# A four-layer gated cross-attention network: one pair of expert reloads issued later, and three transposes moved between products

## The chip, the cores and the metric

The kernel runs on one core of one Trainium2 chip. Its time is device time in microseconds (us), the median of the runs shown. One execution was also recorded by the hardware profiler; every start time below counts from the first instruction of that execution.

A core has five engines that work side by side and wait for each other through semaphores: TensorE (PE in the profile, with its weight loads shown apart as PEld), VectorE (DVE), ScalarE (ACT), GpSimd (POOL) and SyncE (SP), which here issues nearly all transfers. Each engine takes its instructions in the order in which the program was built.

## The reference, cut to what matters

512 tokens (2 batches of 256) of width 256 go through four layers. Each layer adds a cross attention and a feed-forward, each scaled by the tanh of a gate:

```python
x = x + tanh(g_xattn[0]) * L0_xattn(layernorm(x), ctx)
x = x + tanh(g_ffn[0])   * L0_ffn(layernorm(x), ...)        # ternary weights
x = x + tanh(g_xattn[1]) * L1_xattn(layernorm(x), ctx, Wq, Wk, Wv, Wo)
x = x + tanh(g_ffn[1])   * L1_ffn(layernorm(x), w_gate_up, w_down)
x = x + tanh(g_xattn[2]) * L2_xattn(layernorm(x), ctx, ...) # linear attention
x = x + tanh(g_ffn[2])   * L2_ffn(layernorm(x), router_w, gate_w, up_w, down_w)
x = x + tanh(g_xattn[3]) * L3_xattn(layernorm(x), ctx, mask)
x = x + tanh(g_ffn[3])   * L3_ffn(layernorm(x), ...)        # 8 experts, top 2
```

Three of these stages matter here. L1_xattn has 16 heads of width 128: `softmax(q k^T / sqrt(128)) v`, then `@ Wo`. L3_xattn uses the normed tokens as queries against the context itself. L2_ffn sends each token to one of 8 experts:

```python
max_ind = argmax(sigmoid(x @ router_w), axis=1)
for e in range(8):
    h = silu(x @ gate_w[e]) * (x @ up_w[e])
    out = out + where(max_ind == e, h @ down_w[e], 0)
out = out * max_prob
```

## The kernel before, in words

All 512 tokens stay in `x`, four tiles of 128 tokens by 256. A matrix product on TensorE needs the contracted dimension on the partitions, so each normed tile `xn[:, n, :]` is turned: two transposes by TensorE (one for each half of the width) into a small tile `tr`, and one copy by ScalarE into `xT`. There are two buffers for `tr` (pool `ps_tr`), four for ordinary products (`ps_mm`) and two for sums (`ps_acc`).

The order on an engine is largely written by hand. `inline` (line 222) hangs each instruction behind the last one of the same engine's list, so that inside a stage TensorE (`pe_line`), VectorE (`line`) and GpSimd (`pool_line`) follow the text. What is not in a list, ScalarE above all, is placed by the scheduler of the framework.

A product of two fp32 matrices takes two passes. Where it pays, a product is split into cut operands instead: `three` (line 634) makes four products into `same` (two for each half `k` of the contracted width) and two into `cross`.

**Start of the second layer's attention** (lines 773 to 798). The last two value tiles and head 0's keys are multiplied first, while VectorE and GpSimd make the norms. Then `norm_tiles` turns the four tiles with `turned_x`; after the copy of tile 1 it makes head 1's keys for batch 0 (`whole_keys(1, 0)`, two products of 128x512). Head 1's keys for batch 1 follow after the last tile, and then the queries of heads 0 and 1, which read all of `xT`. Between them ScalarE also carries casts for the context's parts (`context_parts`, line 602), which wait for a cut on VectorE.

**Start of the second layer's feed-forward** (lines 1058 to 1136). Tiles 0 and 1 are turned (`turned1`), then `early_products(0)` multiplies the first context tile for the next layer with `three`, which needs nothing of `xT`. Gate and up products of the first batch follow, then tiles 2 and 3, another `early_products`, and the products of the second batch.

**The third layer's experts** (lines 1558 to 1660). Each group of up to 64 tokens of an expert has a fixed place, and the rest of the tokens go into blocks of 32 whose expert is known only when the kernel runs. Six quads of four blocks are multiplied: `l2_up(q)` makes gate and up, `l2_turn` turns the result into `hT`, and `l2_down(q)` multiplies with the ways down. Quads 0 to 3 use the weights of the fixed experts: eight gate/up slabs `gu2[i]` of 1 MB and eight ways down `dn2[i]` of 512 KB. Once quad q has read its two slabs, SP reloads them for the owner of a later block, and likewise `reload_dn2` the ways down:

```python
for i in {0: [0], 1: [1], 3: [3, 2]}.get(q, []):
    reload_dn2(i)
```

Quad 4 reads `gu2[0..3]` and `dn2[0..3]`, and quad 5 `gu2[4..7]` and `dn2[4..7]`. The loop of line 1637 runs one quad ahead: turn q does `l2_up(q)`, then `l2_down(q - 1)`, then `l2_turn` of q, and then some of the homeward products. `homeward` (line 1633) scatters the rows of quad q back to the tokens of tile n by a product with a mask, `l2_back`, summed over the six quads in `y[0]` (tiles 0 and 1) and `y[1]` (tiles 2 and 3).

**Start of the last layer's attention** (lines 1660 to 1753). After the homeward products `l3_stats(n)` adds `y` to `x` and takes the norm, `norm_apply(n)` makes `xn`, `l3_turned(n)` turns it, and `l3_scores` multiplies it with the context. VectorE's list runs: stats 0, stats 1, xn 0, stats 2, xn 1, two small steps on the mask, stats 3, xn 2, xn 3.

Of the kernel before, what the change touches and what calls it, by code (L numbers as in the profile page):

```python
# [30 lines left out]
M = 512  # L31
# [6 lines left out]
QUADS = 6  # L38
# [12 lines left out]
def flamingo(ctx: ExitStack, tc: tile.TileContext, a: dict, out: bass.AP):  # L51
    nc = tc.nc
# [18 lines left out]
    ctxT = turned_ctx.tile([P, B, 2, M], F32, tag="ctxT", name="ctxT")  # L71
# [40 lines left out]
    def load_group(g):  # L112
        w = pair((0, 1, 2, 0)[g], "w1").rearrange("p s c -> p (s c)")
        nc.sync.dma_start(w, a["l1_all"][g])
        return ([w[:, i * 1024 : (i + 1) * 1024].rearrange("p (k c) -> p k c", k=2) for i in range(3)]
                + [w[:, 3072:4096].rearrange("p (h d) -> p h d", d=D)])
# [8 lines left out]
    l1_w = [load_group(0), load_group(1)]  # L125
# [68 lines left out]
    def behind(i, j, reason):  # L194

        tc.add_manual_dep(i.ins, j.ins.name, mybir.DependencyInfo(
            mybir.DependencyClass.NoSync, mybir.DependencyReason.DATA), reason=reason)

    turn = [0]

# [19 lines left out]
    line, pool_line, pe_line = [], [], []  # L220

    def inline(i, line=line):
        if line:
            if line[-1] is not None:
                behind(i, line[-1], "in the order of the text")
            line[:] = [i]
        return i
# [12 lines left out]
    def norm_apply(n, xn, stats):  # L240
        return inline(nc.vector.tensor_scalar(xn[:, n, :], x[:, n, :], *stats, ALU.subtract, ALU.mult))
# [18 lines left out]
    def tokens(t, n):  # L260
        return t[:, n // 2, :, n % 2 * P : (n % 2 + 1) * P]
# [17 lines left out]
    def mm(shape=None):  # L279
        return ps_mm.tile(shape or [P, 512], F32, tag="mm", name="mm")  # L280
# [238 lines left out]
    for s in range(18):  # L519
        n = s // 4  # L520
        if s < 16:
            es[s] = l0_scores(n, s // 2 % 2, s % 2)
        if 1 <= s <= 16:
            m, i, half = (s - 1) // 4, (s - 1) // 2 % 2, (s - 1) % 2
# [8 lines left out]
        if s == 4:  # L533
            behind(nc.scalar.activation(tg, graw, AF.Tanh), exps[-1], "with the table of exponentials")
            p = ps_l0.tile([P, 2, D], F32, tag="s0", name="tot")
# [42 lines left out]
    HD = 128  # L578
# [52 lines left out]
            held.append(diff)  # L631
        return i

    def three(same, cross, left, right):

        for k in range(2):
            for i in range(2):
                inline(nc.tensor.matmul(same, lhsT=left(i, k), rhs=right(i, k), start=(k == 0 and i == 0), stop=(k == 1 and i == 1)), pe_line)  # L638
        for k in range(2):
            inline(nc.tensor.matmul(cross, lhsT=left(2, k), rhs=right(2, k), start=(k == 0), stop=(k == 1)), pe_line)  # L640
# [22 lines left out]
    def value_tiles():  # L663
        return [q4.tile([P, 2, 512], F32R, tag="q4", name="v_parts") for _ in range(3)]
# [4 lines left out]
    def context_tile(mt):  # L669
        return lambda i, k: ctx_parts[i][:, mt // 4, k, mt % 4 * P : (mt % 4 + 1) * P]  # L670
# [97 lines left out]
    def whole_keys(h, b):  # L768
        p = mm()
        chain(p, [(l1_w[0][1][:, k, h * HD : (h + 1) * HD], ctxT[:, b, k, :]) for k in range(2)])  # L770
        nc.scalar.copy(keys[h][:, b * M : (b + 1) * M], p)
# [4 lines left out]
    keys = {h: q4.tile([P, B * M], F32, tag="q4", name="kT") for h in range(2)}  # L776
    for b in range(B):
        whole_keys(0, b)
    xT = q4.tile([P, B, 2, 256], F32, tag="q4", name="xT")

    def turned_x(n, tr):
        nc.scalar.copy(tokens(xT, n), tr)
        if n == 1:
            whole_keys(1, 0)

    for t in (line, pool_line):
        t.append(None)
# [141 lines left out]
    for h in range(16):  # L929
# [9 lines left out]
        for b in range(B):  # L939
# [24 lines left out]
            if h == 14:  # L964
                if b == 0:
                    w_kv2 = value_tiles()
# [13 lines left out]
            if hl and g < 3:  # L980
                n = 2 * (hl - 1) + b
# [62 lines left out]
    def positives(dst, z, t):  # L1044
        inline(nc.vector.scalar_tensor_tensor(dst, z, 0.0, t, ALU.max, ALU.add))

    def early_products(mt):
        same, cross = (ps_acc.tile([P, 512], F32, tag="acc", name="kv2") for _ in range(2))
        three(same, cross, context_tile(mt), lambda i, k: w_kv2[i][:, k, :])
        return same, cross  # L1050

    def early_keys2(mt, same, cross):
# [7 lines left out]
    def turned1(n):  # L1060
        tr = ps_tr.tile([P, 2, P], F32, tag="tr", name="tr")
        for k in range(2):
            inline(nc.tensor.transpose(tr[:, k, :], xn[:, n, k * P : (k + 1) * P], ident), pe_line)
        nc.scalar.copy(tokens(xT, n), tr)

    for n in range(2):
        turned1(n)
    kv0 = early_products(0)
    early_keys2(0, *kv0)
    norm_apply(2, xn, stats1[2])  # L1070
    early_values2(0, *kv0)
# [93 lines left out]
    ctxT = turned_ctx.tile([P, B, 2, M], F32, tag="ctxT", name="ctxT2")  # L1165
# [8 lines left out]
    dn2 = []  # L1174
# [123 lines left out]
    last = norm_stats(NT - 1)  # L1298
# [165 lines left out]
    last = nc.scalar.activation(prob, lgt, AF.Exp, scale=-1.0)  # L1464
# [42 lines left out]
    for n in range(NT):  # L1507
# [9 lines left out]
    _, owners = nc.values_load_multi_w_load_instructions(  # L1517
        owner_i[0:1, :], engines=[mybir.EngineType.SP], min_val=0, max_val=E - 1,
        skip_runtime_bounds_check_because="a count, cut at 7")
# [39 lines left out]

        return 2 * q + j // 2 if q < 4 else 4 * (q - 4) + j  # L1560

    def reload_dn2(q):
        for i in (2 * q, 2 * q + 1):
            nc.sync.dma_start(dn2[i], a["l2_dn_all"][bass.ds(owners[i], 1), :, :].rearrange("e p c -> (e p) c"))

    def l2_up(q):
        pa, pb = mm(), mm()
# [20 lines left out]
    def l2_down(q, hT):  # L1588
        acc = ps_tr.tile([P, D], F32, tag="tr", name="acc2")
        for c in range(4):  # L1590
            for j in range(4):
                inline(nc.tensor.matmul(acc[j * BLK : (j + 1) * BLK, :], lhsT=hT[:, c, j * BLK : (j + 1) * BLK],  # L1592
                                        rhs=dn2[home(q, j)][:, c * D : (c + 1) * D], start=(c == 0), stop=(c == 3)), pe_line)
        for i in {0: [0], 1: [1], 3: [3, 2]}.get(q, []):
            reload_dn2(i)

        top = q1.tile([P, D], F32, tag="q1", name="top2")
        nc.vector.tensor_scalar(top.bitcast(I32), acc.bitcast(I32), -4096, None, ALU.bitwise_and)
        o = kept_back[q][:, 1, :].rearrange("p (i d) -> p i d", i=2) if q < 4 else q2.tile([P, 2, D], F32R, tag="q2", name="o2")
        nc.scalar.copy(o[:, 0, :], top)  # L1600
        nc.vector.tensor_sub(o[:, 1, :], acc, top)
        return o

    last_back = []
# [28 lines left out]
    def homeward(which):  # L1633
        for q, n in which:
            l2_back(q, os[q], backs[q], y, [n])

    for q in range(QUADS + 1):
        if q < QUADS:
            h = l2_up(q)
        if q == 0:  # L1640
            second_rows()
        if 1 <= q <= QUADS:
            backs[q - 1] = l2_mask(q - 1)
            os[q - 1] = l2_down(q - 1, hTs.pop(q - 1))

        if q == 5:
            dn3 = [load(half, f"l3_dn{k}") for k, half in enumerate(halves_of(5, "dn3"))]
            sh = [load(half, f"l3_sh{k}") for k, half in enumerate(halves_of(0, "sh3"))]
            gu3 = [load(half, f"l3_gu{k}") for k, half in enumerate(halves_of(3, "gu3") + halves_of(4, "gu3"))]
        if q < QUADS:  # L1650
            hTs[q] = l2_turn(h)
        if 2 <= q < QUADS:
            homeward([(q - 2, 0)])
        if q == 5:
            homeward([(0, 1), (1, 1)])
        if q == QUADS:
            homeward([(4, 0), (2, 1), (3, 1), (4, 1)])
            load_table(AF.Exp, silus[0], "the table of exponentials")
    homeward([(5, n) for n in range(2)])
    homeward([(q, n) for q in range(QUADS) for n in (2, 3)])  # L1660
    pe_line.clear()
    late = pair(1, "late").rearrange("p s c -> p (s c)")
    shd = late[:, 0 : 6 * D].rearrange("p (c d) -> p c d", d=D)
# [21 lines left out]
    def l3_stats(n):  # L1685
        add_to_x(n, y[n // 2][:, n % 2, :], c2[:, n : n + 1])
        stats3[n] = norm_stats(n)

    def l3_turned(n):
        tr = ps_tr.tile([P, 2, P], F32, tag="tr", name="tr")  # L1690
        for k in range(2):
            inline(nc.tensor.transpose(tr[:, k, :], xn[:, n, k * P : (k + 1) * P], ident), pe_line)
        nc.scalar.copy(tokens(xT, n), tr)
# [39 lines left out]
    l3_stats(0)  # L1733
    l3_stats(1)
    norm_apply(0, xn, stats3[0])
    l3_stats(2)
    norm_apply(1, xn, stats3[1])
    l3_turned(0)
    p = ps_tr.tile([P, B, 4], F32, tag="tr", name="tr")
    chain(p.rearrange("p b c -> p (b c)"), [(ones, named)])  # L1740
    inline(nc.vector.reduce_sum(none, p, axis=AX.X))
# [66 lines left out]
    sent, returned = [], []  # L1808
# [14 lines left out]
    def scatter(table, index, rows, bound, sent):  # L1823
# [2 lines left out]
        for other in sent:  # L1826
            tc.declare_no_dep(i.ins, other.ins, reason="disjoint rows")
        sent.append(i)

    def after_all(read, sent):  # L1830
        for i in sent:
            tc.add_manual_dep(read.ins, i.ins.name, mybir.DependencyInfo(mybir.DependencyClass.Sync, mybir.DependencyReason.DATA),
                              reason="rows of every scatter are read")

    def send3(s):
        full, t = (small.tile([P, 2, E], F32, tag="full3", name="full3", bufs=4) for _ in range(2))
# [16 lines left out]
    def between(ci, b):  # L1853
        if (ci, b) == (0, 0):
            places(place, base3, sel, halves[0])
            send3(halves[0])
            for n in (2, 3):
                l3_turned2(n)
        if (ci, b) == (1, 0):
            for n in (2, 3):  # L1860
                l3_logits(n)
        return (ci, b) in ((0, 1), (4, 1))
# [132 lines left out]
    rows = []  # L1995
    for n in range(NT):
        o = q2.tile([P, 2, D], F32, tag="q2", name="o3g")
        read = (nc.sync, nc.scalar)[n % 2].dma_start(o, yg[n * 2 * P : (n + 1) * 2 * P, :].rearrange("(p k) d -> p k d", k=2))
# [678 lines left out]
```

## Time and profile before

| what | value |
|---|---|
| median of 3 runs | 552.91 us (552.8 to 553.24) |
| the profiled execution's own time | 553.18 us |
| its span, first to last instruction | 551.4 us |
| granted TensorE clock, mean | 0.999 of full speed |
| TensorE matmul busy | 539.8 us, 98% of the span |
| TensorE weight loads busy | 396.1 us, 72% |
| VectorE busy | 333.4 us, 60% |
| ScalarE busy | 237.9 us, 43% |
| GpSimd busy | 123.6 us, 22% |
| moved by transfers | 60.20 MB, mean 109 GB/s |
| reloads of gate/up slabs | 8 of 1024 KB, issued 424.3 to 443.1 |
| reloads of ways down | 8 of 512 KB, issued 432.3 to 452.0 |

A busy share is an average over stages with different limits. A matmul's end is modelled, so a TensorE row that looks full can hide a wait; the idle time in front of a weight load, with its releaser, shows it better. The profile's chain of waits is followed back from the last instruction, at each step to what released it. A transfer's time to landing counts from its issue and includes what is queued in front of it.

### The profile page before, as it was taken

What the parts mean: (1) busy time and instruction counts of PE and PEld (TensorE: products, weight loads), DVE (VectorE), ACT (ScalarE), POOL (GpSimd) and SP (SyncE); (2) the same over time, 40 slices, a digit from 0 to 9 for tenths busy, and PEclk for the clock granted to TensorE, in tenths of its full rate; (3) what the DMA queues carried; (4) which work ended last, traced back from release to release, by engine and by line L of the source; (5) the groups of instructions that cost most, each with busy time, mean ns of one, the idle gap of its engine ahead of it and who ended that gap; (6) DMA issues with size and microseconds to landing.
All of it is one profiled execution on the core that took longest, in us unless ns stands there. A gap on an engine that the chain in (4) does not pass through costs nothing.

```text
span 551.4 us, 8769 instructions
## 1 busy us (share of the span) xinstructions
PE 539.8 (98%) x3322; PEld 396.1 (72%) x3322; DVE 333.4 (60%) x778; ACT 237.9 (43%) x487; POOL 123.6 (22%) x224
## 2 busy tenths in 40 slices
PE   8999999999999999999999999999999989999995
PEld 6554774888888887887888888687776436984464
DVE  5999888645566454755547658664577424563322
ACT  7885565644354434544443533442324212431320
POOL 4776104111030100301012223301031001252150
PEclk9999999999999999999999999999999999999999
DMA  8910120000004000040001204797041999813013
GB/s 277 428 45 0 45 108 1 1 1 0 1 0 153 0 2 1 1 152 1 0 1 37 117 1 162 271 344 311 1 152 40 385 401 249 317 39 128 20 45 130
DMA packets 16104, 60.20 MB, mean 109 GB/s; under 512 B 2717, under 2 KB 5988, under 8 KB 12422
## 3 DMA queue, kind: packets, MB, share of 16 engines
q1 hardware_dynamic: 14294, 54.76, 27.1%
q0 software_dynamic: 1472, 4.28, 2.2%
q8 instruction: 28, 0.46, 0.3%
q10 hardware_dynamic: 288, 0.52, 0.3%
q14 instruction: 22, 0.18, 0.1%
HBM read 54.75 MB, written 5.25 MB: 109 GB/s over the span
## 4 chain that ended last, share of the span: by engine, by line
PE 84%; DVE 5%; DMA 5%; POOL 1%; issue 1%; ACT 1%; SPq 1%; POOLq 0%; DVEq 0%; ACTq 0%
PE mm L284 26%; PE acc L284 18%; PE mm L638 9%; PE mm L640 4%; PE mm L1571 3%; PE q L638 2%; PE mm L1920 2%; DMA gu<-in_l_gu_all 2%; PE s L464 2%; DMA w<-in_l_gate 2%; PE gu L638 1%; PE acc L476 1%; PE outT L715 1%; PE acc L1592 1%; PE q L640 1%
## 5 line engine op out<-in xcount | busy, mean ns | idle before, releaser
L284 PE MATMUL mm<-qT,kT 128*128 128x256 f32 x256 | 60.7, 381 | 0.0
L284 PE MATMUL acc<-e,v 128*128 128x256 f32 x256 | 60.6, 379 | 0.0
L284 PEld LDWEIGHTS mm<-qT,kT 128*128 128x128 f32 x256 | 48.2, 190 | 9.2 <-ACT oT L823 1.6
L284 PEld LDWEIGHTS acc<-e,v 128*128 128x128 f32 x256 | 48.3, 189 | 8.2 <-issue 0.4
L626 POOL TENSOR_TENSOR h_parts<-w,h_top 128x256 fp32r<-128x256 f32 x28 | 20.8, 743 | 140.0 <-PE acc L284 73.6
L812 ACT ACTIVATE e<-mm 128x512 f32<-128x512 f32 x64 | 38.0, 598 | 22.4 <-PE mm L284 22.2
L815 DVE TENSOR_TENSOR t<-e,e 128x512 f32<-128x512 f32 x32 | 22.1, 690 | 24.4 <-ACT e L812 24.2
L468 ACT ACTIVATE e<-s 128x512 f32<-128x512 f32 x64 | 32.9, 606 | 5.9 <-PE s L464 5.7
L236 POOL TENSOR_TENSOR rstd<-mv,eps_ln 128x1 f32<-128x1 f32 x31 | 6.7, 218 | 110.8 <-DVE mv L235 110.7
L643 ACT ACTIVATE v<-mm 128x512 f32<-128x512 f32 x24 | 14.3, 597 | 31.2 <-PE mm L640 31.2
L638 PE MATMUL mm<-ctx_top,h_parts 128*128 128x512 f32 x56 | 27.4, 489 | 0.0
L284 PE MATMUL acc<-w,oT 128*128 128x256 f32 x112 | 26.8, 381 | 0.1
L823 ACT COPY oT<-acc 128x256 f32<-128x256 f32 x32 | 11.9, 372 | 34.2 <-PE acc L284 34.2
L644 DVE SCALAR_TENSOR_TENSOR v<-mm,v 128x512 f32<-128x512 f32 x24 | 16.6, 691 | 16.6 <-ACT v L643 16.6
L643 ACT ACTIVATE kT<-mm 128x512 f32<-128x512 f32 x28 | 16.7, 597 | 20.6 <-PE mm L640 20.6
L287 DVE SCALAR_TENSOR_TENSOR x<-acc,gsum,x 128x256 f32<-128x256 f32 x56 | 23.6, 476 | 2.8 <-PE acc L284 2.2
L1571 PE MATMUL mm<-gu,xsT 128*32 128x512 f32 x192 | 23.4, 596 | 1.4 <-DMA gu<-in_l_gu_all 1.4
L644 DVE SCALAR_TENSOR_TENSOR kT<-mm,kT 128x512 f32<-128x512 f32 x28 | 19.3, 688 | 6.7 <-ACT kT L643 6.7
L284 PEld LDWEIGHTS acc<-w,oT 128*128 128x128 f32 x112 | 20.1, 190 | 3.5 <-ACT oT L823 0.5
L638 PE MATMUL mm<-v_parts,ctx_top 128*128 128x512 f32 x48 | 22.1, 461 | 0.0
L464 PE MATMUL s<-w_q,ctx_nat 32*128 32x256 f32 x256 | 21.6, 401 | 0.5 <-DVE w_q L424 0.2
L638 PE MATMUL mm<-ctx_rest,h_parts 128*128 128x512 f32 x56 | 22.0, 393 | 0.0
(434 smaller groups left out, 1173.2 us busy)
## 6 DMA issues: line engine op xcount, KB each, us to landing
gu<-in_l_gu_all SPq DMA_DIRECT2D x16, 1024.0 KB, 9.1
w<-in_l_all SPq DMA_DIRECT2D x4, 2048.0 KB, 12.4
dn<-in_l_dn_all SPq DMA_DIRECT2D x4, 1024.0 KB, 6.3
dn<-in_l_dn_all SPq DMA_DIRECT2D x8, 512.0 KB, 7.9
gu<-in_l_gu SPq DMA_DIRECT2D x4, 704.0 KB, 14.9
ctxT<-in_ctxT SPq DMA_DIRECT2D x4, 512.0 KB, 13.4
ctx_nat<-in_ctx SPq DMA_DIRECT2D x3, 512.0 KB, 6.2
dn<-in_l_dn SPq DMA_DIRECT2D x2, 704.0 KB
```

Source lines behind the costliest of these rows:

```text
L284: inline(nc.tensor.matmul(dst, lhsT=lhsT, rhs=rhs, start=(i == 0), stop=(i == len(pairs) - 1)), pe_line)
L287: return inline(nc.vector.scalar_tensor_tensor(x[:, n, cols], acc, scalar, x[:, n, cols], ALU.mult, ALU.add))
L464: in_turn(nc.tensor.matmul(ps[j][:, k, :], lhsT=ctx_nat[rows, b, hf, c * P : (c + 1) * P], rhs=qm[rows, n, i, :], start=True, stop=True))
L468: exps.append(nc.scalar.activation(es[j], ps[j], AF.Exp))
L626: nc.gpsimd.tensor_sub(dst[1], src, t)
L638: inline(nc.tensor.matmul(same, lhsT=left(i, k), rhs=right(i, k), start=(k == 0 and i == 0), stop=(k == 1 and i == 1)), pe_line)
L640: inline(nc.tensor.matmul(cross, lhsT=left(2, k), rhs=right(2, k), start=(k == 0), stop=(k == 1)), pe_line)
L643: nc.scalar.mul(dst, cross, -EPS * scale)
L644: return inline(nc.vector.scalar_tensor_tensor(dst, same, (1.0 + EPS) * scale, dst, ALU.mult, ALU.add))
L812: nc.scalar.activation(e, s, AF.Exp)
L815: nc.vector.tensor_add(t, es[0], es[1])
L1571: inline(nc.tensor.matmul(ps[j * BLK : (j + 1) * BLK, :], lhsT=xsT[k][:, (4 * q + j) * BLK : (4 * q + j + 1) * BLK], rhs=gu2[home(q, j)][: ...
```

## The change

It has four parts.

In the experts' loop, the reload of the second pair of ways down (`dn2[2]`, `dn2[3]`) is taken out of `l2_down(1)` and issued in turn 3 of the loop, after `l2_up(3)` has issued its two slabs. It also gets a dependency: SP waits until the homeward product of quad 1 to tile 0 is done. As built, SP's order becomes slabs 0 to 3, ways down 0 and 1, slabs 4 and 5, slabs 6 and 7, ways down 2 and 3, and then ways down 6, 7, 4 and 5 as before. To write this, `after_all` moves from the last layer to the head of the kernel.

At the end of that loop, the last quad's homeward products to tiles 2 and 3 (four products) are taken out of the list and placed behind the last layer's first turn.

In the second layer's attention, head 1's keys for batch 0 are split into their two products, one after each of the turns 0 and 1; they used to follow turn 1 together. As built, ScalarE's copy of turn 1 stands behind the cast `ctx_top` of line 612 instead of ahead of it.

In the second layer's feed-forward, turn 1 is made inside `early_products(0)`, between the first two and the last two products into `same`, by a new argument `between` of `three`.

VectorE's and GpSimd's orders are the same in both kernels.

```diff
+    def after_all(read, sent):
+        for i in sent:
+            tc.add_manual_dep(read.ins, i.ins.name, mybir.DependencyInfo(mybir.DependencyClass.Sync, mybir.DependencyReason.DATA),
+                              reason="only when these are done")
...
-    def three(same, cross, left, right):
+    def three(same, cross, left, right, between=None):
 
         for k in range(2):
+            if k and between:
+                between()
             for i in range(2):
...
+    keys10 = mm()
+
+    def keys_step(k):
+        inline(nc.tensor.matmul(keys10, lhsT=l1_w[0][1][:, k, HD : 2 * HD], rhs=ctxT[:, 0, k, :], start=(k == 0), stop=(k == 1)), pe_line)
+
     def turned_x(n, tr):
         nc.scalar.copy(tokens(xT, n), tr)
+        if n < 2:
+            keys_step(n)
         if n == 1:
-            whole_keys(1, 0)
+            nc.scalar.copy(keys[1][:, 0:M], keys10)
...
-    def early_products(mt):
+    def early_products(mt, between=None):
         same, cross = (ps_acc.tile([P, 512], F32, tag="acc", name="kv2") for _ in range(2))
-        three(same, cross, context_tile(mt), lambda i, k: w_kv2[i][:, k, :])
+        three(same, cross, context_tile(mt), lambda i, k: w_kv2[i][:, k, :], between)
         return same, cross
...
-    for n in range(2):
-        turned1(n)
-    kv0 = early_products(0)
+    turned1(0)
+    kv0 = early_products(0, partial(turned1, 1))
...
-    def reload_dn2(q):
+    def reload_dn2(q, last=None):
         for i in (2 * q, 2 * q + 1):
-            nc.sync.dma_start(dn2[i], a["l2_dn_all"][bass.ds(owners[i], 1), :, :].rearrange("e p c -> (e p) c"))
+            read = nc.sync.dma_start(dn2[i], a["l2_dn_all"][bass.ds(owners[i], 1), :, :].rearrange("e p c -> (e p) c"))
+            if last is not None:
+                after_all(read, [last])
...
-        for i in {0: [0], 1: [1], 3: [3, 2]}.get(q, []):
+        for i in {0: [0], 3: [3, 2]}.get(q, []):
             reload_dn2(i)
...
         if 2 <= q < QUADS:
             homeward([(q - 2, 0)])
+        if q == 3:
+            reload_dn2(1, last_back[0])
...
     homeward([(5, n) for n in range(2)])
-    homeward([(q, n) for q in range(QUADS) for n in (2, 3)])
+    homeward([(q, n) for q in range(QUADS - 1) for n in (2, 3)])
...
     norm_apply(0, xn, stats3[0])
+    l3_turned(0)
+    homeward([(QUADS - 1, n) for n in (2, 3)])
     l3_stats(2)
     norm_apply(1, xn, stats3[1])
-    l3_turned(0)
...
-    def after_all(read, sent):
-        for i in sent:
-            tc.add_manual_dep(read.ins, i.ins.name, mybir.DependencyInfo(mybir.DependencyClass.Sync, mybir.DependencyReason.DATA),
-                              reason="rows of every scatter are read")
```

## The prediction

> **What bounds the kernel now.** I read the engines' busy shares first, then the chain of waits, then the weight loads' waits in the four places that the change touches, and last the transfers' issues and landings around the third layer's experts. TensorE is nearly the whole chain, so a step is worth what it does to TensorE's next instruction:
>
> ```profile
> PE 84%; DVE 5%; DMA 5%; POOL 1%; issue 1%; ACT 1%; SPq 1%; POOLq 0%; DVEq 0%; ACTq 0%
> ```
>
> The chain in order of time (start, length, what) shows the one transfer in the middle of the kernel:
>
> ```profile
> 438.94 3.64 PE mm L1571 x32
> 443.11 11.03 DMA gu<-in_l_gu_all
> 454.18 2.99 PE mm L1571 x25
> ```
>
> The sixth quad's up products start at 451.12 and wait there for the last reloaded gate/up slab, issued at 443.11, landed 11.03 us later. The timeline of weight loads and of ScalarE (start, length, engine, line, what, idle before and its releaser):
>
> ```profile
> 454.18 0.16 PEld L1571 LDWEIGHTS mm<-gu,xsT 128*32 128x32 f32 x8 [2.35 <-DMA gu<-in_l_gu_all]
> ...
> 460.33 0.58 ACT L206 COPY hT<-tr 128x512 f32<-128x512 f32 x1
> ...
> 460.97 1.45 PEld L1592 LDWEIGHTS acc<-dn,hT 128*32 128x32 f32 x32 [0.35 <-ACT hT L206]
> ```
>
> **Edit A, SP's order of the reloads (lines 1562 to 1595 and the quad loop).** Nothing is added or removed in bytes: two issues of 512 KB (0.33 us of SP each) move from 438.14 and 438.71, ahead of the slabs of 442.54 and 443.11, to behind them, with a new wait for the homeward products of the fourth turn of the loop (444.58 + 0.48 = 445.06). Behind that wait on SP stand only the four reloads of 450.39 to 452.00, which wait for TensorE's products ending about 450.3 anyway; they are not delayed. Nothing moves past POOL's queue.
>
> What it gives back at the sixth quad: with quad 4 as the measure (up products 445.00, way down 448.45, so 3.45 us), quad 5 took from 451.12 to 457.22, 6.10 us: 2.65 too many. Two ways down take 2.5 us of the stream (those before landed at 432.26 + 8.1 = 440.4 and 433.23 + 8.4 = 441.6, 1.25 us apart). Without them in front, the last slab lands at 443.11 + 11.0 - 2.5 = 451.6 and its products could begin at 451.12 + 0.33 = 451.45: 0.2 of wait remains, **2.45 us** go.
>
> What is late next is the last quad's own way down. The issues, one at a time (size, us to landing), of 443.11 and of 452.00:
>
> ```profile
> gu<-in_l_gu_all SPq DMA_DIRECT2D x1, 1024.0 KB, 11.0
> ```
> ```profile
> dn<-in_l_dn_all SPq DMA_DIRECT2D x1, 512.0 KB, 8.5
> ```
>
> The last way down lands at 452.00 + 8.5 = 460.5. In the unchanged kernel the products that need it start at 460.97, for ScalarE's copy of hT; 2.45 earlier that copy frees them at 458.5, but the weights come at 460.5. The same bytes stand in one stream that is kept full from 432 to 458 (410 to 440 GB/s in most half microseconds until 451.5), so changing their order does not bring the last of them earlier. The products start at about 460.55: **gain 0.42**, not 2.45. Bounds: the four landings are 455.4, 458.1, 459.3 and 460.5; if the one step of 2.7 us shrinks to 1.3 like its neighbours, 1.4 more is gained (1.8 in all); if the stream loses time, below nothing (the slower rival). I take 0.42, because the stream's slowest part is conserved. The way down of quad 4 needs the moved pair at 451.45 + 3.3 = 454.75; the pair lands 1.25 and 2.5 after 451.6, at 454.1: cover of 0.65.
>
> [...] The row says the stream is full, so early issue of one only delays another; the order of need counts. [...]
>
> **Edit B, the last layer's first turn before four homeward products (lines 1660, 1733 to 1738).** The rows of TensorE's weight loads and VectorE:
>
> ```profile
> 466.26 1.03 PEld L1620 LDWEIGHTS y<-o,back 128*128 128x128 f32 x8
> 466.79 0.40 DVE L241 TENSOR_SCALAR xn<-x,mv,rstd 128x256 f32<-128x256 f32 x1
> 467.31 0.20 PEld L1692 LDWEIGHTS tr<-ident,xn 128*128 128x128 f32 x2
> 467.54 0.48 DVE L287 SCALAR_TENSOR_TENSOR x<-y,c,x 128x256 f32<-128x256 f32 x1 [0.34 <-PE y L1620]
> 468.62 0.38 DVE L241 TENSOR_SCALAR xn<-x,mv,rstd 128x256 f32<-128x256 f32 x1
> 469.14 0.26 PEld L1692 LDWEIGHTS tr<-ident,xn 128*128 128x128 f32 x2
> ```
>
> The eight loads of 466.26 are (4,2), (4,3), (5,2), (5,3). The edit puts the two turns after the fourth, at 466.78. But xn of tile 0 is done at 466.79 + 0.40 = 467.19, and a turn follows its xn by 0.12 (471.35 + 0.41 to 471.88 for the last one): 467.31, as now. TensorE sits idle for 0.53, turns until 467.51, and only then does the four loads (0.52), to 468.03. The scores start at about 468.3 instead of 468.21, as the 0.43 idle ahead of them is now filled. The price is behind it: the sum for tiles 2 and 3 is complete at 468.2 instead of 467.50, so VectorE's add goes from 467.54 to 468.26, **0.72** later; behind it in VectorE's order stands xn of tile 1 (468.62 to 469.34), and the second turn, now at 469.14 and just covered by the scores, comes at 469.34 + 0.38 + 0.14 = 469.86. The third and fourth turns hang on the same VectorE chain. **Cost 0.7**, bounds 0 (if the add is freed by (5,2) alone or the turn's wait is shorter) to 0.75.
>
> **Edit C, head 1's keys cut in two around turn 1 of the second layer (lines 779 to 784).** The four fp32 passes (0.43 each) go half between turns 0 and 1, filling the 0.61 idle before turn 1 at 88.51. But the first queries wait for ScalarE:
>
> ```profile
> 90.47 0.62 ACT L612 CAST ctx_top<-ctx_w 128x512 fp32r<-128x512 f32 x1 [1.11 <-DVE ctx_w L596]
> ...
> 92.20 0.65 ACT L782 COPY xT<-tr 128x256 f32<-128x256 f32 x2
> ...
> 92.90 0.30 PEld L284 LDWEIGHTS q<-xT,w 128*128 128x128 f32 x2 [0.90 <-ACT xT L782]
> ```
>
> As built, the copy of turn 1 (now at 88.99) moves behind the cast of 90.47, which waits for VectorE. [...] Out of order the edit would cost nothing; in order the copy starts at 90.47 + 0.53 = 91.0. It holds one of two turn buffers, so turn 3 goes from about 90.6 to 91.43 and the queries to 91.43 + 1.64 = 93.07; by ScalarE's own count (0.33 for the copy, less the 0.20 it idles before 91.20) they come at 93.03. **Cost 0.15**, bounds -0.1 to 0.45.
>
> **Edit D, turn 1 between the halves of the early products (lines 1047 to 1068).**
>
> ```profile
> 336.11 0.20 PEld L1063 LDWEIGHTS tr<-ident,xn 128*128 128x128 f32 x2 [0.52 <-DVE xn L241]
> ...
> 341.89 0.62 ACT L908 CAST x_two<-x_top 128x512 fp32r<-128x512 f32 x1 [3.23 <-DVE x_top L596]
> ...
> 342.42 0.64 ACT L1064 COPY xT<-tr 128x256 f32<-128x256 f32 x2
> ...
> 343.11 2.02 PEld L284 LDWEIGHTS mm<-xT,ffn 128*128 128x128 f32 x10 [0.29 <-ACT xT L1064]
> ```
>
> Two products (0.23 each) fill the 0.52: TensorE is 0.45 ahead at 337.6. But turn 3 waits for xn of tile 3 (340.20 + 0.86 = 341.06), and the products of 343.11 for the copies of 342.42, which stand on ScalarE behind a cast that VectorE frees; none of that hangs on TensorE. The lead ends as a longer idle at 343.11. **0**, bounds 0.2 gained to 0.1 lost.
>
> **Sum.** -0.42 + 0.7 + 0.15 + 0 = +0.45 on the profiled execution's 553.18 (its span 551.4 and 1.8 around it), which stands 0.27 above the median of 552.91. On the median: 553.4. A difference of 0.2% (1.1 us) is about what a measurement of this kernel can tell from no change, so this is a forecast of no change.
>
> **Rivals.** (1) Faster: quad 5's way down is not bound by the stream, because the late part of it drains quicker once the slabs are gone (350 GB/s from 454 to 457.5 against some 420 earlier leaves room). Then the 2.45 are kept whole: 552.91 - 2.45 + 0.85 = 551.3. Against it: the landing of 460.5 is 2 us too late for it. Chance 0.14. [...] Chance 0.27. (3) That the change doesn't do what it says is inside the forecast: C and D fill their waits and give it back, chance of the forecast 0.59.
>
> The forecast's own range is 552.3 to 554.0; with the rivals 551.6 to 554.6. Of the forecast's 0.59, 0.02 falls past each side, so faster 0.16, same 0.55, slower 0.29.
>
> **What would show it.** A: the wait of 2.35 at the sixth quad gone, and a new wait of about 2 us for dn before the last way down, with the start near 460.5. B: 0.5 idle before the first turn, the second at +0.7 relative to the end of the homeward products. C: queries near 93.05. D: products of 343.11 unmoved relative to the attention's end. I am wrong if no wait for dn appears (rival 1), or if dn lands after 461.2 (rival 2).

## The result, and the profile after

The changed kernel took 555.27 us (median of 19 executions, 553.66 to 559.39), the kernel before, run beside it, 553.17 (19 executions, 552.34 to 554.22). The ratio is 1.0048 with a 95% interval of 1.003 to 1.0067: slower by half a percent, 2.1 us in the medians, where 553.4 and no change had been forecast.

The profiled execution of the changed kernel is one of its short ones: 553.85 us, span 552.1, mean granted clock 0.997. It is 0.67 above the profiled execution of before, close to the forecast sum of 0.45, and yet ten of the nineteen executions lie 1.4 to 5.5 us above it. So there are two questions: whether the sum was right by its terms, and what makes so many executions longer than the one in the profile.

The chain of waits of the kernel after, in the experts' stage (start, length, what):

```profile
452.10 8.70 DMA dn<-in_l_dn_all
460.81 0.04 issue
460.85 1.93 PE acc L1607 x30
```

The transfer on the chain is no longer a slab of the sixth quad but the last way down, issued at 452.10. The timeline of weight loads and of ScalarE (start, length, engine, line, what, idle before and its releaser):

```profile
452.31 0.16 PEld L1586 LDWEIGHTS mm<-gu,xsT 128*32 128x32 f32 x8 [0.94 <-DMA gu<-in_l_gu_all]
...
458.47 0.58 ACT L211 COPY hT<-tr 128x512 f32<-128x512 f32 x1
459.10 0.14 PEld L1607 LDWEIGHTS acc<-dn,hT 128*32 128x32 f32 x2 [0.35 <-ACT hT L211]
460.85 1.45 PEld L1607 LDWEIGHTS acc<-dn,hT 128*32 128x32 f32 x30 [1.61 <-DMA dn<-in_l_dn_all]
...
467.17 0.20 PEld L1709 LDWEIGHTS tr<-ident,xn 128*128 128x128 f32 x2 [0.49 <-issue]
467.34 0.54 PEld L1635 LDWEIGHTS y<-o,back 128*128 128x128 f32 x4
...
469.70 0.20 PEld L1709 LDWEIGHTS tr<-ident,xn 128*128 128x128 f32 x2 [0.61 <-issue]
```

Read against the rows of before: the wait of 2.35 at the sixth quad is 0.94, hT is there 1.87 earlier (459.10 and 460.97), and nearly all of that comes back as the wait of 1.61 in front of the last way down, which starts in earnest at 460.85. In the last layer the first turn stands at 467.17 as before, with 0.49 idle ahead of it and the four homeward products behind it, and the second turn slides from 469.14 to 469.70.

Why the last transfer comes no earlier is seen in the windows of one microsecond (window, its length, busy time of each engine, granted clock, busy share of the transfer engines, GB/s). The kernel before:

```profile
446.00:447.00 1.00, 1.00 (x16) 0.27 (x10) 0.00 (x0) 0.01 (x1) 0.00 (x0) 1.00 1.06 418
...
453.00:454.00 1.00, 0.00 (x0) 0.00 (x0) 0.00 (x0) 0.00 (x0) 0.00 (x0) 1.00 1.23 324
454.00:455.00 1.00, 0.82 (x8) 0.29 (x12) 0.00 (x0) 0.00 (x0) 0.00 (x0) 1.00 0.83 311
```

The kernel after:

```profile
445.00:446.00 1.00, 1.00 (x14) 0.31 (x15) 0.29 (x1) 0.85 (x2) 0.00 (x0) 1.00 1.02 270
446.00:447.00 1.00, 1.00 (x16) 0.37 (x12) 0.00 (x0) 0.00 (x0) 0.00 (x0) 1.00 0.69 279
...
453.00:454.00 1.00, 1.00 (x12) 0.26 (x8) 0.00 (x0) 0.00 (x0) 0.00 (x0) 1.00 1.03 414
454.00:455.00 1.00, 1.00 (x16) 0.35 (x12) 0.00 (x0) 0.73 (x2) 0.00 (x0) 1.00 1.03 422
```

In these two executions each kernel has one thin place in its stream. Before, it lies at 453 to 456 us (311 to 336 GB/s), where the slabs run out and the last four ways down have only just been issued; after, it lies at 445 to 447 (270 and 279), where the moved pair used to be queued. In neither is the queue empty: the ways down of 450.39 to 452.00 are under way in the one, the slabs of 442.64 and 443.20 in the other. From 443 to 457 us both move the same, 392 and 389 GB/s on average. The move exchanged one thin place for another.

### The profile page after: what moved, and what is told of

The parts are those of the page before. It is cut to its first block, busy times and chain, and to the rows that moved or that the text cites. A ratio compares the mean times of both kernels' runs of the same rounds, so it can differ in the third digit from the quotient of the medians.

```text
span 552.1 us, 8766 instructions
## 1 busy us (share of the span) xinstructions
PE 540.1 (98%) x3322; PEld 396.4 (72%) x3322; DVE 333.2 (60%) x778; ACT 237.9 (43%) x487; POOL 123.5 (22%) x224
```

## The experiments

The kernel before took 553.2 to 555.6 us (medians) on the chips that served these runs, so each kernel is compared only with before of its own group. The label "A" is the moved pair of ways down, "B" the last layer's first turn, "C" and "D" the two turns of the second layer.

**First group: which edit?** Theory S puts the scatter on A, theory T on one of the turns.

```diff
 e1_no_A: the kernel after, with
-        for i in {0: [0], 3: [3, 2]}.get(q, []):
+        for i in {0: [0], 1: [1], 3: [3, 2]}.get(q, []):
...
-        if q == 3:
-            reload_dn2(1, last_back[0])
```

> The kernel after with the ways down of the second pair issued where they were before (behind the second quad's way down, no wait on a homeward product); the three turns stay moved. Theory S (the moved ways down leave the stream of the experts' weights with no slack, so that in many executions the last slab or the last way down lands several us late): the executions draw together again, within about 1.5 us of each other as before's do, and the median is before's plus what the turns cost (+0.72 and +0.15): about 554.0, ratio 1.001 to 1.002. Theory T (one of the moved turns makes the executions scatter): half of them stay 2 to 5 us above the lowest, median about 555 to 555.5, ratio 1.003 to 1.005.

Measured: 554.35 (13 executions, 553.75 to 556.19) against 553.32, ratio 1.0021 (1.0011 to 1.0032). B, C and D together cost 1.03 and bring little scatter: two of the thirteen lie over 556.

```diff
 e2_A_only: the kernel before, with
-        for i in {0: [0], 1: [1], 3: [3, 2]}.get(q, []):
+        for i in {0: [0], 3: [3, 2]}.get(q, []):
...
+        if q == 3:
+            reload_dn2(1, last_back[0])
```

> The kernel before with the ways down of the second pair moved behind the homeward product, its wait with it, and no turn moved. Theory S: the scatter is here, lowest about 552.5 to 552.8 (before less up to 0.4), half of the executions 2 to 5 us above that, median 554 to 555. Theory T: no scatter, all within 1.5 us, median about 552.8 (before less 0.42).

Measured: 556.14 (5 executions, 554.29 to 557.01), ratio 1.0047 (1.0032 to 1.0062). The scatter is here, and stronger than forecast.

The same without SyncE's wait, `reload_dn2(1)`:

> As the one before, without SyncE's wait for the homeward product: the two ways down stand at the same place in SyncE's order, but are issued as soon as their buffers are free. Theory S by the wait (the wait itself sets the late landing): no scatter, time as before or up to 0.4 below. Theory S by the order alone (the slabs of the fifth and sixth quads run ahead of these ways down and the last ones come later): the same scatter as with the wait. Theory T: no scatter with or without it.

Measured: 554.06 (14 executions, 552.26 to 557.45), ratio 1.0016 (1.0001 to 1.0032). Scatter again, with a lower middle; the order alone suffices for it. The wait put the two issues at 445.08 and 445.61 instead of 444.00 and 444.53.

> The kernel after itself, beside the others on the same chip and with one more profile. Both theories: lowest 553.7 to 554.0, about half of the executions 2 to 5 us above, ratio 1.003 to 1.007. If its profile falls on one of the longer executions: theory S expects the added time between 445 and 462 us of the span, as TensorE's wait for a slab or a way down; theory T expects it in the second layer's attention or between 467 and 475 us.

Measured: 555.58 (22 executions, 552.22 to 559.53), ratio 1.0036 (1.0022 to 1.005). Theory T falls: the scatter belongs to A.

**Second group: why does A scatter?** The moved pair frees the sixth quad earlier, and with it the buffers into which SyncE loads the last layer's weights. In the kernel before these loads are issued from 457.83, in e2_A_only from 456.92, in the kernel after from 455.96, each time while the last ways down are still in flight. Theory C says that this collision delays the last way down; theory R that the transfer engines, starting again out of the thin place at 445 us, stay behind unevenly. The next kernels hold those loads, eight of them (the expectations call them six), until TensorE has begun the last way down:

```diff
-        if q == 5:
-            dn3 = [load(half, f"l3_dn{k}") for k, half in enumerate(halves_of(5, "dn3"))]
+        if q == QUADS:
+            dn3 = [load(half, f"l3_dn{k}", down_first) for k, half in enumerate(halves_of(5, "dn3"))]
...
     def load(half, name, held=()):
...
+        if held:
+            after_all(read, held)
```

(`down_first` is the fourth product of the last `l2_down`; the two `sh` and four `gu` loads are held like the two `dn`. As built, a load of 640 KB for the shared expert, `late`, now goes ahead of the held ones: in f1_A_l3_held it was issued at 457.58, before the last way down had landed.)

> The kernel before with only the ways down of the second pair moved, as in e2_A_only (554.29 to 557.01, median 556.14), and besides this the six loads of the last layer's weights held on SyncE until the last way down's fourth product is done. Theory C (collision: the moved pair empties the sixth quad's stall, so these six loads start about 1 to 2 us earlier and share the transfer engines and the memory with the last packets of the last way down, which took 0.25 to 0.33 us instead of 0.16 in the profile of e2_A_only): the scatter goes, the executions lie within about 2 us, median 552.5 to 553.3, the last way down lands at about 460 us of the span. Theory R (restart: the engines run dry at 444.5 us and start the sixth quad's slabs unevenly, so that one of them stays behind for good): the scatter stays, median above 554.5, last way down again at 461 to 462.5.

Measured: 554.36 (12 executions, 552.61 to 555.77) against 554.44, ratio 1.0 (0.9991 to 1.001). Weight loads of its profile:

```profile
452.20 0.16 PEld L1580 LDWEIGHTS mm<-gu,xsT 128*32 128x32 f32 x8 [0.95 <-DMA gu<-in_l_gu_all]
...
459.80 1.45 PEld L1603 LDWEIGHTS acc<-dn,hT 128*32 128x32 f32 x30 [0.68 <-DMA dn<-in_l_dn_all]
```

The wait for the slab is the 0.94 of the kernel after, and the wait for the last way down is 0.68 instead of 1.61.

> The kernel after, all four edits, with the same six loads held in the same way. Theory C: median 553.3 to 554.1 (before plus the turns' 0.9 less up to 0.4), highest below 556. Theory R: as the kernel after, median 555 to 555.6, highest near 559.

Measured: 554.80 (11 executions, 553.83 to 555.79), ratio 1.0008 (0.9999 to 1.0017): with the eight loads held, the four edits together cost about 0.4 us, and no execution lies more than 1.4 above the median of before.

> The kernel before with the same six loads held and nothing else changed. Both theories: as before within 0.3 us, since there the loads start at 457.8 and almost nothing of the last way down is left when their packets come (0.2 MB of theirs before its last packet); under theory C perhaps a smaller highest time. If the held loads cost time later in the last layer, it shows here: above 553.6.

Measured: 554.68, ratio 1.0006 (0.9998 to 1.0015). Holding by itself brings nothing to the kernel before.

The fourth kernel fills both thin places with one of the two ways down each:

```diff
-            reload_dn2(i)
+            reload_dn2(i, (0,) if i == 1 else (0, 1))
...
+        if q == 3:
+            reload_dn2(1, (1,))
```

> The kernel before with one of the two ways down moved (the second of the pair, behind the eighth slab, no wait on a homeward product), the other left in front of the slabs. The stream should run dry neither at 444.5 (512 KB are still queued there, 1.2 us) nor at 452 us (512 KB are queued there too). Theory R: the stream ends about 0.9 us earlier and without scatter, median 552.3 to 553. Theory C: the sixth quad's stall shrinks by about 1.2, the last layer's loads start earlier by as much, and the scatter is half of that of e3_A_no_wait, median 553.5 to 554.

Measured: 554.01 (11 executions, 553.27 to 554.62), ratio 0.999 (0.9981 to 0.9999). Weight loads of its profile:

```profile
453.03 0.16 PEld L1571 LDWEIGHTS mm<-gu,xsT 128*32 128x32 f32 x8 [1.58 <-DMA gu<-in_l_gu_all]
```

The sixth quad waits 1.58 for its slab, and the last way down, which starts at 459.81 instead of 460.97, waits for no transfer at all. In the microseconds from 443 to 457 its lowest rate was 340 GB/s, against 311 before and 270 after.

**Third group: the same on one chip, and a collision made on purpose.**

> The kernel e2_A_only once more, now beside the held one on the same chip, because e2_A_only gave few executions and f1_A_l3_held ran on a chip on which the kernel before took 1.1 us more. Theory C and theory R alike: scatter, median 1.5 to 3 us above before on this chip, highest 3 to 5 above.

Measured: 556.08 (12 executions, 553.98 to 559.93) against 555.39, ratio 1.0023 (1.0002 to 1.0043).

> The kernel f1_A_l3_held once more. Theory C (the last layer's six loads, not the moved pair itself, make the last way down late): median within 0.4 us of before on this chip and at least 1.2 us under g1_A_only. Theory R (engines restarted unevenly at 444.5 us stay behind): the same as g1_A_only within 0.5 us.

Measured: 554.46 (12 executions, 552.91 to 557.4), ratio 0.9987 (0.9972 to 1.0003): 1.6 us under g1_A_only on the same chip, which speaks for theory C, but with two executions above 557.

> The kernel f4_half_A once more, to see whether its 0.4 us under before hold on another chip: 0.2 to 1.0 us under before; theory C allows for a few executions 1 to 2 us higher.

Measured: 553.96 (12 executions, 553.35 to 555.62), ratio 0.9977 (0.9966 to 0.9988). On this chip half of A is 1.4 us under before. Its profile still has a thin place, 328 GB/s at 455 us.

The collision on purpose, in the kernel before:

```diff
-            dn3 = [load(half, f"l3_dn{k}") for k, half in enumerate(halves_of(5, "dn3"))]
             sh = [load(half, f"l3_sh{k}") for k, half in enumerate(halves_of(0, "sh3"))]
-            gu3 = [... halves_of(3, "gu3") + halves_of(4, "gu3") ...]
+            gu3 = [... halves_of(3, "gu3") ...]
+            dn3 = [load(half, f"l3_dn{k}") for k, half in enumerate(halves_of(5, "dn3"))]
+            gu3 += [... halves_of(4, "gu3") ...]
```

> The kernel before with the order of the last layer's loads changed: the two shared ones and the first two of the experts' come first, since their buffers are free from 449 us on, so that 2.8 MB are issued from 452.5 us, right behind the last way down, instead of from 457.8. Nothing of the second pair is moved. Theory C: the collision is now in the kernel before: the last way down lands 1 to 3 us later than 460.5, with scatter, median 1 to 3 us above before. Theory R, or transfers that are served strictly in the order of issue: the last way down lands as in the kernel before, time within 0.3 us of it, no scatter.

Measured: 554.55 (11 executions, 553.42 to 556.82), ratio 0.9988 (0.9975 to 1.0001). In its profile the last way down landed at 462.58, 2.8 behind the one ahead of it, as theory C had it; by time theory C missed.

**Fourth group: a long execution caught in the profile.**

> The kernel before, profiled on the chip of these runs, so that what the chip adds (before took 553.3, 554.4 and 555.4 us on three chips) can be told from what a change adds. On a chip where it takes 554 or more, the time behind the last way down should be 91 to 92.5 us instead of 90.43, and the eighth slab's wait near 2.35 us again.

Measured: 555.15, span 553.4. The wait for the slab is 2.35, the last way down starts at 460.80, and 92.6 us follow instead of 90.4. This chip's extra time lies behind the experts, half of it (1.1) after the last product of the shared expert has begun.

> The kernel after once more, for one more profile. Both theories: if this execution is a long one (over 556), the added time stands before TensorE's last way down, in its two waits for transfers (the eighth slab's and the last way down's), which together took 2.55 us in the profile at 553.85; in a long one 4.5 us and more. If the two waits stay near 2.6 in an execution over 556, both theories are wrong about the place.

Measured: 558.82, span 557.0, mean granted clock 0.994.

```profile
455.06 0.16 PEld L1586 LDWEIGHTS mm<-gu,xsT 128*32 128x32 f32 x8 [2.41 <-DMA gu<-in_l_gu_all]
...
464.04 1.45 PEld L1607 LDWEIGHTS acc<-dn,hT 128*32 128x32 f32 x30 [1.94 <-DMA dn<-in_l_dn_all]
```

Against h4_before_look the experts begin 1.48 later (422.64 and 421.16), the last way down 3.24 later, and the span is 3.6 longer. So 1.76 us came in this stage, as two waits of 4.35 together. The 1.48 before it have another cause, in the windows of this execution:

```profile
403.78:407.19 3.41, 3.41 (x32) 3.39 (x31) 2.32 (x12) 1.08 (x4) 1.41 (x2) 1.00 0.95 303
407.19:410.61 3.42, 3.23 (x10) 2.28 (x11) 2.33 (x9) 0.71 (x2) 0.00 (x0) 0.50 0.76 311
410.61:414.02 3.41, 3.41 (x16) 2.73 (x15) 3.02 (x10) 0.00 (x0) 0.89 (x2) 1.00 0.00 0
```

The granted clock (third number from the end) was 0.50 for 3.41 us.

> The kernel e2_A_only once more, for one more profile: the same as for the one before (its two waits were 2.01 and 1.85 us at 554.29 us).

Measured: 558.07, span 556.4, clock 0.994. The weight loads, then the windows:

```profile
459.12 0.14 PEld L1599 LDWEIGHTS acc<-dn,hT 128*32 128x32 f32 x2 [0.35 <-ACT hT L211]
461.92 0.20 PEld L1599 LDWEIGHTS acc<-dn,hT 128*32 128x32 f32 x8 [2.66 <-DMA dn<-in_l_dn_all]
...
465.23 0.30 PEld L1627 LDWEIGHTS y<-o,back 128*128 128x128 f32 x2 [0.55 <-issue]
```

```profile
458.08:461.49 3.41, 1.52 (x10) 0.83 (x8) 0.88 (x3) 0.89 (x2) 0.11 (x1) 1.00 0.98 222
461.49:464.90 3.41, 2.98 (x27) 1.37 (x30) 0.00 (x0) 0.00 (x0) 0.00 (x0) 0.50 1.00 235
464.90:468.32 3.42, 3.42 (x31) 3.05 (x26) 2.04 (x6) 0.41 (x1) 0.02 (x1) 1.00 1.04 227
```

The way down lands at 461.9 and TensorE waits 2.66 us for it. In the window that holds most of that wait its matmuls are busy for 1.52 of 3.41 us, and in the next window the granted clock is 0.50: the products that took 1.85 us up to the homeward ones in the kernel after (460.85 to 462.70) now take 3.31. Against h4_before_look the way down starts 1.1 us later (0.35 of it brought along from before the experts), and the products behind it take 1.46 more: in this execution the late landing and the halved clock come together.

> The kernel before with one way down of the second pair moved behind the eighth slab (as g3_half_A, which took 0.9977 of before) and the last layer's six loads held until the last way down's fourth product. Theory C: the loads no longer meet the last way down's last packets, so the few executions 1 to 2 us higher go as well, and the median is 0.1 to 0.5 us under g3_half_A's ratio (0.997). Theory R: nothing is gained by holding, ratio 0.9977 to 0.999.

Measured: 554.26 (12 executions, 553.14 to 556.03) against 555.55, ratio 0.9975 (0.9965 to 0.9985), the same as g3_half_A: holding adds nothing to half of A.

**Fifth group.**

> The kernel g4_before_l3_early once more: the kernel before with 2.8 MB of the last layer's weights issued right behind the last way down. In its first profile the last way down landed at 462.6 us and TensorE waited 1.00 us for it, as theory C has it, and yet its median was 0.84 us under before. Theory C by place: the last way down lands 2 to 3 us behind the one ahead of it again (1.2 to 1.3 in the kernel before) and a wait of 0.5 to 2 us stands at it. Theory C by time: median above before. If the median is under before again, the collision is there but does not set the median in this order.

Measured: 554.42 (11 executions) against 554.29, ratio 1.0007 (0.9998 to 1.0016). This time the last way down landed at 460.2, 1.3 behind the one ahead, and nothing waited for it.

```diff
 i2_B_only: the kernel before, with
     norm_apply(0, xn, stats3[0])
+    l3_turned(0)
+    homeward([(QUADS - 1, n) for n in (2, 3)])
     l3_stats(2)
     norm_apply(1, xn, stats3[1])
-    l3_turned(0)
```

(and the two pairs taken out of the loop's last homeward list)

> The kernel before with edit B alone: the first turn of the last layer goes ahead of the last two homeward pairs. The forecast's term: 0.72 us more than before, ratio 1.0013, the four turns' starts further apart by that, no scatter beyond before's. If B cost nothing the ratio would be within 0.0005 of 1.

Measured: 554.97 (11 executions, 554.57 to 555.42), ratio 1.0013 (1.0004 to 1.0022), 0.68 over before. Its turns:

```profile
467.34 0.20 PEld L1701 LDWEIGHTS tr<-ident,xn 128*128 128x128 f32 x2 [0.50 <-issue]
...
469.87 0.20 PEld L1701 LDWEIGHTS tr<-ident,xn 128*128 128x128 f32 x2 [0.61 <-issue]
```

The last way down starts at 460.99, 0.02 from that of before, and the second turn at 469.87 instead of 469.14: 0.73 later, as are the third and the fourth.

**What the groups say together.** Take the landing of the last way down behind the one ahead of it (issue plus time to landing). With before's order it is 1.3 to 1.4 us in all five profiles that have it. With A and the loads free to start it is 2.1 to 3.2 in all seven: after, e2, e3, e4, g1, h2, h3. With A and the loads held it is 1.2 in all three. In e2_A_only it is a few packets that are late: 95% of the last 128 packets of the ways down had ended at 459.6 and the last one at 461.5, in f1_A_l3_held at 459.0 and 459.3. In h3_A_only_look the last packet had ended at 460.2, and the landing still came at 461.9. So with before's order of loads the late landing came only with A, and with A whole, holding the loads took it away. That sharing the transfer engines by itself is the cause is not shown: with early loads and before's order it came once (2.8) and once not (1.3), and half of A gave 1.4 and 3.2, and 2.4 with the loads held.

The same landing can be counted from the issue of the stage's first slab, which takes out what came before the stage. It is 35.2 to 36.2 us with before's order, 36.4 to 38.4 in the seven profiles with A and the loads free, and 35.5 to 35.6 with A and the loads held; in the kernel before, the products that need it start at 36.7. Not all of this lateness can be the collision's. In e2, e3 and h2 the second way down of the moved pair had already landed 31.5 to 32.0 us after that first issue, against 30.3 to 30.9 in the seven other profiles with A whole, free or held, and none of the last layer's loads had been issued by then. So theory R is not ruled out as a part of it. Why one execution has it and the next not stays open.

The clock tells a part. Of the 72 executions with A and free loads (h2 and h3 left out) 18 had a mean granted clock of 0.995 or less, which is what 3.41 us at 0.50, as in h3, would leave of 0.998 (an estimate: 1.7 of 553 us); they took 3.8 us more than before's median on average, the other 54 took 1.3 more. With A alone it was 10 of 31, with 3.4 more, and 0.35 for the other 21. The mean clock of the 18 is 0.994, which by the same estimate stands for some 2 us against 0.998, so the clock is not all of it, and two of the longest executions of the changed kernel, 558.38 and 559.24, kept 0.999 and 0.996. Of 151 executions of before in the five groups 2 had such a clock, of 35 with A and the loads held 2, of 35 with half of A none. How many of the 18 lost their clock at the last way down, as h3 did, and how many elsewhere, as h2 did, no run shows.

## Why the prediction was wrong, point by point

**The stall at the sixth quad** was said to lose 2.45. From the start of its up products to the last of them it takes 4.13 us in the profile after (451.22 to 455.35) instead of 6.10, so it lost 1.97; in h3 about as much, in h2, counted to the turn of hT against h4_before_look, 0.4. Without the pair in front, the slabs start out of a thin stream, and the two landings of 1.25 us each that the step subtracted are not wholly saved. The stall itself was larger than the 2.65 worked out: to the turn of hT quad 4 takes 5.30 (445.00 to 450.30) and quad 5 takes 8.34 (451.12 to 459.46).

**The last way down at 452.00 + 8.5 = 460.5, gain 0.42.** This is the step that failed: A was booked as a gain of 0.42, and it cost time. B, C and D together measured 1.03, which by subtraction leaves A about 1.1 of the 2.1; alone it measured 0.7 (g1_A_only) and 2.8 (e2_A_only, five executions).

In the profile the last way down landed at 460.80 and the products began at 460.85; allowing for the 0.09 by which the experts' stage began later, the gain is 0.2. So "the stream's slowest part is conserved" held in the mean and in the short executions. But the step took one execution's landing for a constant. Counted from the first slab's issue, its 460.5 is 36.2, the latest of the five profiles with before's order, and the seven with A and free loads have 36.4 to 38.4; that the short ones come close to it is in part luck. Nor was the stream full: it moved 311 to 336 GB/s at 453 to 456 us.

The step also made the last transfer of the stream the thing that TensorE waits for and left no slack behind it: in the kernel before, a slab with 6.8 us of products behind it was awaited, and the last way down had 0.4 to spare (1.5 in h4_before_look). In long executions it landed at 461.9 (h3) and 464.00 (h2, of which 1.48 came from earlier), which is beyond the 461.2 named for rival 2. Rival 2, the slower one, had the right place and the right outcome; that the clock would be halved behind the landing, as in h3, was not reckoned with. That the stream runs thin where the moved pair used to be queued is not by itself shown to be the price: with the loads held the thin place stays (287 GB/s at 445 us in f1_A_l3_held), and the way down lands as early as with before's order.

**The order of need** was right for the short executions (the products of the last way down begin at 460.85 in the profile, 460.97 before) and wrong for the median, 2.1 us up. Half of A, with one of the two issued early and one in the order of need, won 0.4 to 1.4 us.

**The cover of 0.65 for quad 4's way down** held: the pair landed at 453.6 and 454.8, and no wait for it appears there.

**SyncE's wait delays nothing behind it**: so it was, but the wait itself moved the pair 1.1 us further back than its place in the order would have; without it the ratio was 1.0016 instead of 1.0047. The 1.0047 comes from only five executions, and on another chip the kernel with the wait measured 1.0023, so what the wait costs is not shown.

**What a faster sixth quad sets off** was not asked. The last layer's loads start when the sixth quad's buffers come free, so they moved forward by 1.9 us in the profile, onto the last way down. Holding them took 1.6 us off A's median on one chip.

**Edit B, 0.72**: measured alone 0.68 (0.0013 of the time, interval 0.0004 to 0.0022), by the mechanism named: the second turn 0.73 later.

**Edit C, 0.15, bounds -0.1 to 0.45**: the rows of ScalarE in the kernel after:

```profile
90.19 0.62 ACT L617 CAST ctx_top<-ctx_w 128x512 fp32r<-128x512 f32 x1 [1.66 <-DVE ctx_w L601]
90.72 0.37 ACT L794 COPY xT<-tr 128x256 f32<-128x256 f32 x1
91.13 0.20 PEld L260 LDWEIGHTS tr<-ident,xn 128*128 128x128 f32 x2 [1.36 <-ACT xT L794]
```

The copy does stand behind the cast and starts 0.53 after it, as booked, and the last turn waits 1.36 for it. The first scores start at 96.13 instead of 96.01, in an execution whose turn 0 was 0.28 earlier: 0.1 to 0.4, inside the bounds. B, C and D together measured 1.03, B alone 0.68, so some 0.35 is left for C and D, less than the intervals can tell apart.

**Edit D, 0**: the products after the turns start at 343.18 with 0.53 idle ahead of them (0.29 before). The lead ended as a longer idle, as forecast.

## What to carry to other kernels

A move that takes a stall off one transfer can hand it to the next one in the queue; ask whether that one has slack. Here the last way down landed 1.2 to 3.2 us behind the one ahead of it, and one profiled execution doesn't show such a spread. Ask also what the freed buffers let start, and hold that behind the transfer that is now awaited, or move only half: one of the two ways down moved took 0.999, 0.9977 and (with the loads held) 0.9975 of before, and beats both kernels. Read the granted clock behind a wait as well: in h3, behind the wait of 2.66 us, it was 0.50 for 3.41 us.

## What was not expected of the hardware

The granted clock fell in the middle of h2 and h3. In h3 it was 0.50 for 3.41 us (461.49 to 464.90), behind the window with most of the 2.66 us wait, in which matmuls were busy for 1.52 of 3.41 us by the record, a share of 0.45. Nearly the same share went without it in g1_A_only: 1.58 of 3.41 from 459.07, in an execution whose mean clock of 0.998 leaves no room for 3.41 us at 0.50 (they would take 0.003 off; an estimate). The share of 0.58 (1.97 of 3.42, from 451.55) in which the kernel before has its 2.35 us stall was followed by a window at 1.00 (454.97 to 458.38).

In h2 the clock was 0.50 from 407.19 to 410.61, behind a window in which matmuls were busy throughout by the record, with 31 weight loads in 3.41 us. So the recorded share alone does not tell when the clock falls, and what it depends on, no run shows.
